# Loading the values of a cross-attention kernel in runs of 80 rows per head instead of 77

## The chip, the cores and the metric

The kernel runs on one core of a Trainium2 chip. The core has a matrix engine (TensorE, "PE" in the profile; its weight loads are "PEld"), a vector engine (VectorE, "DVE"), a scalar engine (ScalarE, "ACT"), a general engine (GpSimd, "POOL"), and SyncE ("SP"), which in this kernel computes nothing and issues every DMA. Sixteen DMA engines carry the transfers. The metric is device time of one execution in microseconds (us), the median of several runs.

## The reference

Only the text part of the original block is alive: `x` is 32 batches of 512 queries with 640 channels, `ctx` is 32 batches of 77 keys with 1024 channels, and there are 20 heads of 32 channels.

```python
q = _heads(x @ to_q_w)                    # 32 x 20 x 512 x 32
k = _heads(ctx[:, :77] @ to_k_w)          # 32 x 20 x 77 x 32
v = _heads(ctx[:, :77] @ to_v_w)
p = softmax(q @ k.T / sqrt(32))           # 512 x 77 for each head
out = _merge(p @ v) @ to_out_w + to_out_b + x
```

The three other attentions of the original (object, others, image prompt) read slices of `ctx` that are empty here, so they add nothing.

## The kernel before, in words

Every matmul is made in three passes: each operand is split into a high and a low part (`split`, lines 98 to 100: ACT copies the high part, DVE subtracts it to get the low part), and high times high, high times low and low times high are added up.

**First stage, to about 289 us.** Keys and values of all 32 batches are computed (matmuls in lines 163 and 189). All 2464 rows (32 times 77) lie one behind the other. Both results go to scratch memory in DRAM: `k_dram`, and `v_dram`, which holds for each row, head and channel the high and the low part side by side. This stage's instructions, its DMAs too, are placed by the scheduler.

**Main stage.** Work is cut into 160 blocks `n = 5 b + j`: batch `b` (512 queries) and chunk `j` of four heads. `slot(n)` (line 485) writes out by hand what PE, ACT, DVE and POOL do while block `n` is the newest one in the pipeline, and the text below calls this "slot j" of a batch. In slot `n`:

- PE makes the scores of block `n` in four parts (`sc`, line 334), between them the queries of block `n+1` (`pq`, line 316), then the product of probabilities and values for block `n-3` (`pa`, line 415), then, in slots 2, 3, 4 and 0 of a batch but not in slot 1, the output projection of a quarter of an earlier batch (`po`, line 442).
- ACT makes the 16 exponentials of block `n` (`pn`, line 352), the high parts of queries and results (`qt`, `at`, line 99), the high part of the probabilities of block `n-2` (`pp`, lines 395 and 399), and in slots 3 and 0 of a batch the high parts of `x` (`xt`, line 267).
- DVE takes maxima (`nm`, line 342), low parts (`pp`, line 396; line 100), and transposes blocks of 32 by 32 (`z`, line 371). POOL normalizes (`pn`, line 364), makes further low parts (`pp`, line 400; `xt`, line 268) and adds the bias to the residual (`xr`, line 437).

The probabilities have queries on partitions and must have keys there. The transposed blocks `z` go to a DRAM buffer `pd` in four DMAs (line 378), and come back as `raw` in two (lines 387 and 388). There is **one** `raw` buffer: the load for a block can only be issued when POOL and DVE have finished with the block before it, and when that block's four `pd` stores have landed. `split_p` then makes `pp` from `raw`: ACT line 395, DVE line 396, ACT line 399, POOL line 400. `pa` consumes `pp`.

**The values.** A head's 77 keys are padded to 80 in `pn` (the three columns stay zero), so four heads fill 320 rows: two tiles of 128 and one of 64. `vb` holds the values in the same layout, as a block diagonal in three tiles; it is cleared once. `SEGMENTS` (lines 35 to 43) lists for each tile which rows of which head go there: runs of 77, 48, 29, 77, 16 and twice 61 rows (the last run is stored twice, for the high and for the low part of the probabilities). `load_values(b, g)` (line 298) issues one DMA for each run, for two chunks (`g = 0`) or three (`g = 1`); a row and chunk is 256 bytes. It is called from `refill`, behind the `pa` of slots 2 and 4. `load_keys` fetches `kb` likewise, in four DMAs.

**Order of the DMAs.** All DMAs go through one queue, SP's, which takes them one after the other and waits in front of each for what it needs. A DMA also waits until the one eight places ahead of it has landed, because completion semaphores are used in turn. Up to slot 7, SP's order is the program's; from slot 8 on the scheduler places SP's instructions by its own estimate of times, while the other engines keep the order written in `slot`. In steady state the order of one batch is, from slot 0: `kb` x4, `vb` x7 of `g = 0`, `xr`, `raw` x2, `out`, `pd` x4, `xr`, `raw` x2, `out`, `pd` x4, `xr`, `kb` x4, `vb` x2 of `g = 1`, `raw` x2, `pd` x4, `vb` x5, `out`, and on to slots 3 and 4.

Of the kernel before, what the change touches and what calls it, by code (L numbers as in the profile page):

```python
# [8 lines left out]
F32 = mybir.dt.float32  # L9
FPR = mybir.dt.float32r  # L10
# [12 lines left out]
P = 128  # L23
Q = 32
HEADS = 20
HD = 32
NKEY = 77
HPC = 4
KCOLS = HPC * NKEY
KPAD = 80  # L30
# [5 lines left out]
for _t in range(3):  # L36
    for _i in range(HPC):
        _lo = max(_t * P, _i * KPAD)
        _hi = min((_t + 1) * P, _i * KPAD + NKEY)
        if _lo < _hi:  # L40
            SEGMENTS.append((_t, _lo - _t * P, _i, _lo - _i * KPAD, _hi - _lo))
            if _t == 2:
                SEGMENTS.append((_t, _lo - _t * P + 64, _i, _lo - _i * KPAD, _hi - _lo))
# [6 lines left out]
def kernel(  # L50
# [24 lines left out]
    nc = tc.nc  # L75
    B, S, C = x.shape
    CA = ehs.shape[2]
    NT = B * NKEY
# [11 lines left out]
    dram = ctx.enter_context(tc.tile_pool(name="scratch", bufs=1, space=DRAM))  # L90

    k_dram = dram.tile([P, NC_, 2, NT], FPR, name="k_dram")
    v_dram = dram.tile([NT, HEADS, HD, 2], FPR, name="v_dram")
    wo_dram = dram.tile([P, NC_, 2, C], FPR, name="wo_dram")

    bias = const.tile([P, C], F32, name="bias")
# [111 lines left out]

    zero = kvt.tile([P, G], FPR, name="zero", tag="craw")
    nc.vector.memset(zero.bitcast(F32), 0.0)  # L210
    warm = psk.tile([P, G], F32, tag="ps", name="warm")
    for _ in range(12):
        nc.tensor.matmul(warm, zero[:, :P], zero, start=True, stop=True)
# [473 lines left out]
```

## Time and profile before

The median is 2141.44 us over three runs (2139.94 to 2143.78). The profiled execution took 2144.53 us by itself; its span, from the first to the last instruction, is 2142.8 us, at a mean granted TensorE clock of 0.985.

| what | us | share of the span |
| --- | --- | --- |
| PE busy | 2020.4 | 94% |
| PE weight loads busy | 1793.9 | 84% |
| ACT busy | 1359.8 | 63% |
| DVE busy | 1337.6 | 62% |
| POOL busy | 1094.8 | 51% |
| DMA queue of SP, share of 16 engines | | 71.5% |

Matmuls overlap in the pipeline, so a busy PE is not yet a PE at its peak. A row of waits reads: engine, tile and line that waited, what ended the wait, then us in total, number of waits and the longest. A row of the timeline reads: start and duration in us, engine, line, operation, tile written and tile read, how many instructions are merged, and in brackets the engine's idle time in front of it with what ended it. "SPq" is SyncE's queue issuing a DMA; its duration is the time to issue, waiting included, not the transfer.

### The profile page before, as it was taken

The page shows a single profiled execution, that of the slowest core. Times are in us where ns is not written, and L with a number is a line of the kernel's source. Part 1 is how long each engine was busy: PE and PEld are TensorE (multiplying, and loading weights), DVE is VectorE, ACT ScalarE, POOL GpSimd, SP SyncE. Part 2 cuts the span into 40 slices and gives each one's busy share as a digit, 9 for nine tenths or more (in the row PEclk, how much of TensorE's full clock was granted, in tenths as well). Part 3 has the DMA queues.
Part 4 walks back from the last instruction along what each step waited for, and adds up shares of the span by engine and source line. Part 5 has one row for each costly group of instructions (what it writes and reads, how often), then busy time and mean ns, then how long its engine had stood idle before and what let it go on. Part 6 is the DMA issues. An engine that isn't in the chain of part 4 may idle for free.

```text
span 2142.8 us, 36233 instructions
## 1 busy us (share of the span) xinstructions
PE 2020.4 (94%) x11012; PEld 1793.9 (84%) x11012; DVE 1337.6 (62%) x1872; ACT 1359.8 (63%) x6057; POOL 1094.8 (51%) x618
## 2 busy tenths in 40 slices
PE   8899995899999999999999999999999999999997
PEld 7799974788888888888888888888888888888886
DVE  5433244467677677666667666767767767666663
ACT  3321145577677777677767777767777677777662
POOL 0000043456656566665666665656656656666653
PEclk9999998899999999999999999999999999999998
DMA  7953265677777777777777777777777777777664
GB/s 190 266 181 115 92 138 148 192 200 205 205 206 206 209 202 204 199 213 213 211 201 202 211 211 198 204 200 207 206 197 206 206 212 206 208 202 201 189 186 129
DMA packets 524241, 416.43 MB, mean 194 GB/s; under 512 B 138480, under 2 KB 427760, under 8 KB 524048
## 3 DMA queue, kind: packets, MB, share of 16 engines
q1 hardware_dynamic: 524048, 414.13, 71.5%
q8 instruction: 88, 1.44, 0.3%
q14 instruction: 105, 0.86, 0.1%
HBM read 238.69 MB, written 175.31 MB: 193 GB/s over the span
## 4 chain that ended last, share of the span: by engine, by line
DMA 30%; ACT 23%; PE 19%; SPq 10%; issue 8%; DVE 7%; POOL 3%; DVEq 0%; POOLq 0%; ACTq 0%
ACT pn L352 14%; DMA pd<-z 12%; DMA raw<-pd 8%; DMA xs<-in_x_dram 6%; PE pk L163 5%; PE pv L189 5%; ACT pp L395 3%; PE po L442 3%; SPq L378 3%; SPq L303 3%; DVE nm L342 2%; PE pq L316 2%; PE pa L415 2%; SPq L433 2%; DVE z L371 2%
## 5 line engine op out<-in xcount | busy, mean ns | idle before, releaser
L352 ACT ACTIVATE pn<-sc,nm 128x77 f32<-128x77 f32 x2560 | 814.2, 363 | 295.9 <-DVE nm L342 295.8
L316 PE MATMUL pq<-xt,wq_s 128*128 128x512 f32 x2400 | 639.1, 396 | 10.0 <-POOL xt L268 8.9
L364 POOL TENSOR_TENSOR pn<-pn,rs 128x1232 f32<-128x1232 f32 x160 | 387.0, 2419 | 471.2 <-DVE rs L363 424.9
L352 ACT ACTIVATION_READ_ACCUMULATOR pn<-sc,nm 128x1 f32 x2560 | 620.5, 243 | 0.0
L442 PE MATMUL po<-wo_s,at 128*128 128x320 f32 x3840 | 587.8, 310 | 3.5 <-DVE xr L458 2.1
L442 PEld LDWEIGHTS po<-wo_s,at 128*128 128x128 f32 x3840 | 569.3, 188 | 7.3 <-DVE xr L458 2.9
L316 PEld LDWEIGHTS pq<-xt,wq_s 128*128 128x128 f32 x2400 | 429.9, 189 | 76.4 <-POOL xt L268 11.6
L396 DVE TENSOR_TENSOR pp<-raw,pp 128x1024 fp32r<-128x1024 f32 x160 | 307.0, 1919 | 228.2 <-ACT pp L395 228.1
L334 PE MATMUL sc<-kb,qt 128*128 128x308 f32 x1920 | 389.5, 309 | 27.3 <-ACT qt L99 20.7
L415 PE MATMUL pa<-pp,vb 128*128 128x512 f32 x1280 | 343.4, 405 | 59.4 <-DVE pp L396 33.8
L334 PEld LDWEIGHTS sc<-kb,qt 128*128 128x128 f32 x1920 | 327.0, 189 | 85.6 <-ACT qt L99 28.4
L400 POOL TENSOR_TENSOR pp<-raw,pp 64x512 fp32r<-64x512 f32 x160 | 295.6, 1848 | 156.3 <-ACT pp L399 137.1
L415 PEld LDWEIGHTS pa<-pp,vb 128*128 128x128 f32 x1280 | 244.7, 198 | 132.8 <-DVE pp L396 53.2
L395 ACT CAST pp<-raw 128x1024 fp32r<-128x1024 f32 x160 | 174.9, 1093 | 214.1 <-DMA raw<-pd 211.0
L342 DVE TENSOR_REDUCE nm<-sc 128x4 f32<-128x308 f32 x640 | 291.8, 460 | 7.8 <-PE sc L334 5.3
L371 DVE STREAM_TRANSPOSE z<-pn 128x1280 f32<-128x1280 f32 x160 | 240.2, 1501 | 25.5 <-POOL pn L364 23.7
L268 POOL TENSOR_TENSOR xt<-xs,xt 128x512 fp32r<-128x512 f32 x160 | 204.2, 1286 | 96.6 <-ACT xt L267 86.8
L437 POOL TENSOR_TENSOR xr<-xr,bias 128x640 f32<-128x640 f32 x128 | 201.0, 1570 | 53.1 <-DMA xr<-in_x_dram 43.5
L100 DVE TENSOR_TENSOR at<-pa,at 128x512 fp32r<-128x512 f32 x160 | 110.7, 692 | 140.8 <-ACT at L99 140.8
L100 DVE TENSOR_TENSOR qt<-pq,qt 128x512 fp32r<-128x512 f32 x160 | 110.2, 689 | 64.6 <-ACT qt L99 64.3
L163 PE MATMUL pk<-ct,wk_s 128*128 128x512 f32 (+1 forms) x600 | 137.4, 390 | 10.9 <-ACT ct L99 10.8
L189 PE MATMUL pv<-wv_s,ct 128*128 128x320 f32 (+1 forms) x960 | 142.1, 309 | 0.0
(37 smaller groups left out, 1109.9 us busy)
## 6 DMA issues: line engine op xcount, KB each, us to landing
pd<-z SPq DMA_DIRECT2D x640, 160.0 KB
raw<-pd SPq DMA_DIRECT2D x160, 512.0 KB
xs<-in_x_dram SPq DMA_DIRECT2D x128, 320.0 KB
xr<-in_x_dram SPq DMA_DIRECT2D x128, 320.0 KB
out_dram<-xr SPq DMA_DIRECT2D x128, 320.0 KB
raw<-pd SPq DMA_DIRECT2D x160, 128.0 KB
v_dram<-vs SPq DMA_DIRECT2D x19, 640.0 KB
k_dram<-ks SPq DMA_DIRECT2D x20, 512.0 KB
```

Source lines behind the costliest of these rows:

```text
L163: nc.tensor.matmul(pks[j][:, :gn], wk_s[:, k, a, j * P : (j + 1) * P], cts[k][:, c, :gn], start=(k == 0 and n == 0), stop=(k == NK - 1 and ...
L189: nc.tensor.matmul(pv[:tn, :HALF], cts[k][:, a, t0 : t0 + tn], wv_s[:, k, c, h * HALF : (h + 1) * HALF], start=(k == 0 and n == 0), stop=( ...
L316: nc.tensor.matmul(pqs[n], wq_s[:, k, a, j * P : (j + 1) * P], xts[b, k][:, c, :], start=(k == 0 and m == 0), stop=(k == NC_ - 1 and m == 2),)
L334: nc.tensor.matmul(sc[:, :KCOLS], qt[:, a, t * P : (t + 1) * P], kb[:, c, :], start=(m == 0), stop=(m == 2),)
L342: nc.vector.tensor_reduce(nm, sc[:, :KCOLS].rearrange("p (h k) -> p h k", k=NKEY), AX.X, ALU.max, negate=True)
L352: nc.scalar.activation(pnb[n % 2][:, at, :NKEY], sc[:, i * NKEY : (i + 1) * NKEY], AF.Exp, bias=nm[:, i : i + 1], accum_out=sms[n][:, at : ...
L364: nc.gpsimd.tensor_tensor(pf, pf, rs.unsqueeze(2).to_broadcast([P, NQ * HPC, NKEY]), ALU.mult)
L371: nc.vector.transpose(z.rearrange("p b t j -> p t b j"), pn.rearrange("p (t h) k -> p t (h k)", t=NQ).rearrange("p t (b i) -> p t b i", i=Q),)
L396: nc.vector.tensor_tensor(pp[:, 2:4, :], raw[:, 0:2, :], pp[:, 0:2, :].bitcast(F32), ALU.subtract)
L400: nc.gpsimd.tensor_tensor(pp[64:, 4, :], raw[:64, 2, :], pp[:64, 4, :].bitcast(F32), ALU.subtract)
L415: nc.tensor.matmul(pas[n], vb[:, t, :, a], pp[:, c, :], start=(m == 0), stop=(m == len(PASSES) - 1),)
L442: nc.tensor.matmul(po[:, :HALF], ats[b * NC_ + j][:, a, t * P : (t + 1) * P], wos[0][:, j, c, h * HALF : (h + 1) * HALF], start=(j == 0 an ...
```

## The change

The runs of `SEGMENTS` end at the padded length, 80, in place of 77: they become 80, 48, 32, 80, 16 and twice 64 rows. The three extra rows of a run are the first three rows of the next batch, and they are multiplied by the zero columns of the probabilities. Behind the last batch there is no next one, so `v_dram` grows by three rows, and one DMA at the start writes zeros to them, from the tile `zero` that is there for warming up PE.

```diff
 for _t in range(3):
     for _i in range(HPC):
         _lo = max(_t * P, _i * KPAD)
-        _hi = min((_t + 1) * P, _i * KPAD + NKEY)
+        _hi = min((_t + 1) * P, (_i + 1) * KPAD)
         if _lo < _hi:
@@
-    v_dram = dram.tile([NT, HEADS, HD, 2], FPR, name="v_dram")
+    v_dram = dram.tile([NT + KPAD - NKEY, HEADS, HD, 2], FPR, name="v_dram")
@@
     nc.vector.memset(zero.bitcast(F32), 0.0)
+    nc.sync.dma_start(
+        v_dram[NT:].rearrange("n h d a -> (n h d a)").rearrange("(p u) -> p u", u=P).bitcast(F32),
+        zero[: (KPAD - NKEY) * HEADS * HD * 2 // P, :P].bitcast(F32),
+    )
```

The number of DMAs is the same but for the zeros. The order on ACT and POOL is the same; on DVE too; on PE six projection matmuls move ahead by a few places once, at slot 8. SP's order changes: the zeros come behind the first two DMAs of the start, and in every batch the `xr` load that stood between `vb` of `g = 0` and `raw` moves behind `raw` x2 and `out`.

## The prediction

> **What bounds the kernel now.** I read the page's busy shares first, then the waits, then the timeline of one batch.
>
> ```profile
> PE 2020.4 (94%) x11012; PEld 1793.9 (84%) x11012; DVE 1337.6 (62%) x1872; ACT 1359.8 (63%) x6057; POOL 1094.8 (51%) x618
> ...
> PEclk9999998899999999999999999999999999999998
> ```
>
> PE is the busiest by far. To see what is left above its own speed I took the distances between starts of successive matmuls in the trace: median 231 ns for `pq`, 142 for `sc`, 229.5 for `pa`, 147 for `po`. A batch has 75, 60, 40 and 120 of them: 17.3 + 8.5 + 9.2 + 17.6 = 52.7 us. It takes 55.6 us (blocks 10 to 155: 1613.5 us over 29 batches). So PE stands still for 2.97 us a batch. By slot, the excess over those medians is 0.1 in slot 0, 0.9 in slot 1 (`sc`), 1.9 in slot 2 (`pa` 1.3, `sc` 0.6), 0.0 in slot 3, 0.1 in slot 4. Only slots 1 and 2 have anything to give: 2.8 us a batch. The waits say who is behind them:
>
> ```profile
> ACT pp L395 <- DMA raw<-pd: 211.0, 77, 8.1
> ...
> PEld pa L415 <- DVE pp L396: 53.2, 44, 2.6
> ...
> PE pa L415 <- DVE pp L396: 33.8, 37, 2.3
> ...
> PE sc L334 <- ACT qt L99: 20.7, 28, 1.2
> ```
>
> PE waits for `pp` and `qt`, thus for DVE and ACT; ACT waits 211 us for `raw`. The timeline of batch 12 (slot 0 starts at 982.23, slot 1 at 993.68, slot 2 at 1001.69) shows the place:
>
> ```profile
> 985.22 1.77 POOL L400 TENSOR_TENSOR pp<-raw,pp 64x512 fp32r<-64x512 f32 x1 [2.19 <-ACT pp L399]
> 985.37 3.55 SPq L303 DMA_DIRECT2D vb<-v_dram  x7
> ...
> 988.97 2.04 SPq L433 DMA_DIRECT2D xr<-in_x_dram  x1
> ...
> 991.12 0.39 SPq L387 DMA_DIRECT2D raw<-pd  x1
> ...
> 995.81 1.05 ACT L395 CAST pp<-raw 128x1024 fp32r<-128x1024 f32 x1 [3.49 <-DMA raw<-pd]
> ...
> 1001.69 0.55 PE L334 MATMUL sc<-kb,qt 128*128 128x308 f32 x2 [0.81 <-ACT qt L99]
> ...
> 1008.37 1.90 PE L415 MATMUL pa<-pp,vb 128*128 128x512 f32 x7 [0.95 <-DVE pp L396]
> ```
>
> The `raw` buffer is free when POOL ends at 986.99, and the last of its `pd` stores landed at 986.32. Yet `raw` is issued at 991.12: SP is held up by `vb` (the last of the seven takes 1.20 us to issue) and by `xr`, which takes 2.04 us where other `xr` issues take 0.35 to 0.53 us. No landing that `xr` waits for falls there: the DMA eight places ahead, a `kb`, landed at 987.01. ACT, done with slot 0 at 992.3, stands idle 3.49 us, and is that late for slot 1 and for the `pp` of slot 2. Slot 1 has no projection, so PE needs just 7.2 us in it, and ACT cannot catch up.
>
> **Why those issues are slow.** The trace's updates of the DMA semaphores give each landing. From the end of issue, median over the batches, `vb` with `g = 1` takes: 48 rows 1.5 us, 77 rows 2.2, 16 rows 2.1, 29 rows 3.1, 61 rows **4.5**; with `g = 0`: 1.6, 1.8, 1.55, 2.1 and **3.7**. Fewer bytes take longer. The number of updates tells why: the other 1793 DMAs give 16 each, 28,688 in all. The trace holds 32,656, so 124 a batch remain for the 14 loads of `vb`. That is exactly what comes out if 48 and 16 rows use 16 DMA engines, 77 rows 11, and 29 and 61 rows one (k updates and one more where k is below 16: 4 x 12 + 4 x 16 + 6 x 2 = 124). The Trainium skill, "DMA: Bandwidth & Descriptors", section "Why a DMA increments its semaphore by 16 and not by 1", has the rule: the largest k up to 16 that divides both sides' slowest dimension. The trace agrees to the last update. A packet of 256 bytes takes 18 ns in the trace; two runs of 61 rows and three chunks are 366 packets on one engine, an estimated 6.6 us, and SP can't issue on while that engine's queue is full.
>
> **The change part by part.**
>
> *Runs of 80, 48, 32, 80, 16, 64, 64 rows*: all divide by 16, so all use 16 engines. The seven of `g = 0` are 768 packets, 48 an engine, 48 x 18 ns = 0.9 us. Issue: seven at 0.3 to 0.42 us (the rows of 48, 77 and 16), 2.7 us in place of 3.55 in the printed row, and `xr` without its 2.04. The padding adds 75 packets a batch, 75 x 18 ns / 16 = 0.08 us of DMA, hidden: DMA engines are busy 71.5%.
>
> *`raw` ahead of `xr` and `out`*: in batch 12 it goes out at 985.37 + 2.7 = 988.1 in place of 991.12, 3.0 us earlier; in batch 9 (7.91 after slot 0's start, `vb` from 2.23) 2.9 earlier, in batch 18 (8.58, `vb` from 2.60) 3.2. It waits for its eighth predecessor, the last `kb`, landed at 987.01, and for POOL at 986.99; both are over. `xr` goes to 989.5 and lands before 993; it is wanted by POOL two slots later (26 us after slot 0's start): hidden.
>
> *Walk from there*: landing takes 3.5 (the low quarter) to 4.2 us; I take 4.0 from the end of issue: 992.4. ACT is free at 992.3, so its wait goes and all that follows on ACT is 3.3 us earlier. In batch 9's terms (slot 1 at 11.45, slot 2 then at 18.65): ACT `pp` at 10.4 and not 12.59; `pp` 1.66 and `xt` 1.24, exponentials from 13.3, `qt` at 16.6, complete at 17.9, before 18.65: the `sc` stall goes. The next `raw` waits for POOL (13.9, was 16.05) and for `pd` (its four go out from 6.8, were 9.54; landed about 12, were 15.69), lands about 18; ACT ends slot 1 at 18.96, DVE's `pp` (2.75 us) ends at 22.8, and `pa`, which needs it from its second matmul at 23.6, doesn't wait. So 2.8 us go; margins are 0.7 to 0.8 us, so I leave 0.3 us a batch as residue: 2.5 us. Batches 2 to 31 have the pattern: 30 x 2.5 = **75 us**.
>
> *Once, in slot 9*: there `vb` (398.41 on) is followed by a `raw` issue of 2.92 us at 403.36, landing at 409.84; with 2.7 us for `vb` it goes out at 401.1 and lands at about 405.2. PE's wait of 7.31 us for `xt` at 415.44 hangs on it: **4.6 us**. Slots 5 and 6 (32 us of stalls) keep theirs: SP waits there for POOL, not for `vb`.
>
> *Zeros*: third on SP at the start. They wait for the memset (0.91 to 1.39), when SP is busy with the first two anyway, and cost one issue, 0.45 us, and a place among eight: up to 2 us if the fourth `cs` must wait for the first landing (4.49). I take **1 us** lost, as the first keys hang on `cs`. PE's six moved matmuls: their inputs are ready (`at` complete at 391.4), nothing.
>
> Two rules for the whole. "DMA: Bandwidth & Descriptors", "Rules for kernel authors", says that transfers under 64 KB pay mostly overhead; all of `vb` is under 58 KB. By that rule the runs would land as before, and the change be worth 0. The row is against it: 45.8 KB in runs of 61 land in 4.5 us, 57.8 KB in runs of 77 in 2.2. I go by the row.
>
> Sum: 75 + 4.6 - 1 = 79 us. The profiled execution itself was 2144.5, so it would be 2065.5; from the median of the runs, 2141.4, **2062 us**.
>
> **The rivals.**
> *Half the gain (17 in 100)*: ACT or DVE becomes the bound in slot 1. ACT needs 8.56 us from one `pp` to the next there, PE 7.2. For it: margins of 0.8 us, and `raw` landing times reach 5.3 us at the upper quarter over all slots. If `raw` lands 1.5 us later than I say, half of the 2.8 us stays: 30 x 1.4 + 2.3 - 1 = 43 us, 2098 us. Against: nothing slow lies ahead of it any more.
> *No change (5 in 100)*: `raw` isn't held by `vb` at all, or the new runs don't spread; then 2141 us. Against: two conditions are over 4 us before the issue.
> *Slower (7 in 100)*: PE, now without pauses, is granted less clock. Half clock for 3.4 us (the unit in which the trace grants it) costs 1.7 us; more than 1.6 such a batch outweigh 2.65 us gained. Three a batch give 5.1, and 30 x 2.45 = 74 us slower: 2215 us. For it: nothing in a row. The trace has clock 0.5 in 342 to 421 and at 2097, next to stalls, and 1.0 from 80 to 342 where PE is full. The skill's "TensorE: Matmul & The Clock Gate", Part 1, says the same way round that idleness throttles; only a power limit would do it.
>
> **How the numbers follow.** The full gain has 71 in 100. Its own range: all stalls of slots 1 and 2 gone (84) and slot 9's 9.9 gone gives 2047; twice my residue and nothing in slot 9 gives 2076. The range runs down to 2044 and up to 2108, past the half-gain case. Faster by over 0.2% (about what a measurement can tell): 71 + 17 = 88; same 5; slower 7.
>
> **What would show it.** Landing of the 64-row runs falls from 4.5 and 3.7 us to about 2; updates per DMA become 16 throughout, 3,520 more packets of 4 bytes and 2,400 more of 256, so the queue's 524,048 packets become about 530,000. The `xr` issue of 2 us vanishes, `raw` follows `vb` at once, ACT's wait for `raw` falls from 211 us to under 110, PE's waits for `pp` from 87 us to under 20, a batch takes 53 us. I am wrong if `raw` lands no earlier despite an earlier issue, if ACT's wait turns into one for `nm` or `qt`, or if the granted clock falls below 0.98.

## The result and the profile after

The changed kernel takes 2092.7 us (median of four runs, 2090.7 to 2094.4) against 2140.7 for the kernel before (four runs). The ratio is 0.9774, with a 95% interval from 0.9757 to 0.9791: 48 us, 2.3%, faster. I had forecast 2062 us and a gain of 79 us. The direction holds and the range holds the time, but only because it was drawn past the rival "half the gain"; that case came, to which I had given 17 in 100, and not the full gain with 71.

The page of the kernel after, its head and its queue:

```profile
span 2092.2 us, 36233 instructions
...
PE 2006.4 (96%) x11012; PEld 1795.0 (86%) x11012; DVE 1346.8 (64%) x1872; ACT 1363.7 (65%) x6057; POOL 1108.3 (53%) x618
...
q1 hardware_dynamic: 530013, 414.77, 73.4%
```

The span shrank by 50.6 us. By the starts of the score matmuls, 7.0 us of that lie before block 10 (4.8 of them in slot 9), 40.9 between blocks 10 and 155, and the rest behind. A batch takes 54.23 us in place of 55.64; I had forecast 53. The queue's packets are as forecast: 524,048 + 2,400 of 256 bytes + 3,520 of 4 bytes + 45 for the zeros = 530,013. So every run now uses 16 DMA engines.

The waits of the kernel after (engine, tile and line, what ended the wait, us in total, how often, the longest). The line numbers are five higher than before:

```profile
ACT pp L400 <- DMA raw<-pd: 145.6, 66, 7.8
...
PEld pa L420 <- DVE pp L401: 43.5, 35, 2.6
...
PE pa L420 <- DVE pp L401: 28.2, 32, 2.3
```

ACT waits for `raw` 145.6 us where it was 211.0; I had said under 110. PE's wait of 20.7 us for `qt` (`sc <- ACT qt`) is no longer among the larger waits. But PE still waits for `pp`: 71.7 us in the two rows, where it was 87.0. I had said under 20.

The timeline of batch 12 of the kernel after; slots 0, 1 and 2 start at 963.24, 974.69 and 981.72:

```profile
966.13 3.65 SPq L308 DMA_DIRECT2D vb<-v_dram  x7
...
969.89 0.53 SPq L392 DMA_DIRECT2D raw<-pd  x1
...
975.09 1.05 ACT L400 CAST pp<-raw 128x1024 fp32r<-128x1024 f32 x1 [1.66 <-DMA raw<-pd]
...
983.66 1.16 ACT L400 CAST pp<-raw 128x1024 fp32r<-128x1024 f32 x1
...
984.85 2.76 DVE L401 TENSOR_TENSOR pp<-raw,pp 128x1024 fp32r<-128x1024 f32 x1 [0.68 <-ACT pp L400]
...
986.51 0.40 PE L420 MATMUL pa<-pp,vb 128*128 128x512 f32 x1
```

ACT's idle time before the first `pp` is 1.66 us (3.49 before), and slot 1 takes 7.03 us, which is all PE's own. But the second `pp`, for the `pa` of slot 2, starts at 983.66 and DVE ends it at 987.61, while PE has come to `pa` at 986.51 and can do only the one matmul that needs no low part.

This table is worked out from the traces: medians over batches 2 to 30, in us. "Time" is the median of the kernel's own runs; the kernel before, run beside each of them, had medians from 2139.7 to 2147.3, so small differences are to be read from the ratios below. "`raw` landed" is the landing of the first of the two loads. "PE's stalls" are the excess over the matmul distances of the prediction, a mean for a batch. "Issue behind vb" is how long SP took to issue the DMA next behind the seven `vb` of `g = 0`.

| kernel | time | `raw` issued, from slot 1's start | `raw` landed | ACT `pp`, from slot 1 | ACT `pp`, from slot 2 | stalls slot 1 | stalls slot 2 | issue behind `vb` |
|---|---|---|---|---|---|---|---|---|
| before | 2140.7 | -3.15 | 1.80 | 1.88 | 2.67 | 0.90 | 1.92 | 2.00 |
| after | 2092.7 | -4.99 | -0.55 | -0.48 | 2.16 | 0.04 | 1.38 | 0.53 |
| only 61 to 64 | 2092.5 | -5.29 | -0.83 | -0.67 | 2.00 | 0.05 | 1.35 | 0.53 |
| 61 kept, others 80 and 32 | 2155.7 | -2.78 | 2.43 | 2.50 | 2.68 | 1.39 | 1.91 | 2.11 |
| 78 | 2096.6 | -5.30 | 0.39 | 0.47 | 2.14 | 0.05 | 1.43 | 0.44 |
| 79 | 2228.8 | -1.58 | 3.36 | 3.44 | 2.68 | 2.28 | 1.95 | 0.36 |
| no `vb` loads | 2090.5 | -6.57 | -2.31 | -1.47 | 1.93 | 0.04 | 1.27 | |

### The profile page after: what moved, and what is told of

It is laid out like the page before. It is cut to its first block, busy times and chain, and to the rows that moved or that the text cites. A ratio compares the mean times of both kernels' runs of the same rounds, so it can differ in the third digit from the quotient of the medians.

```text
span 2092.2 us, 36233 instructions
## 1 busy us (share of the span) xinstructions
PE 2006.4 (96%) x11012; PEld 1795.0 (86%) x11012; DVE 1346.8 (64%) x1872; ACT 1363.7 (65%) x6057; POOL 1108.3 (53%) x618
## 4 chain that ended last, share of the span: by engine, by line
PE 34%; ACT 23%; DMA 19%; DVE 8%; issue 6%; SPq 5%; POOL 3%; DVEq 0%; POOLq 0%; ACTq 0%
ACT pn L357 16%; DMA pd<-z 10%; PE po L447 9%; PE pq L321 6%; PE pk L164 6%; PE pv L190 5%; PE pa L420 5%; DMA xs<-in_x_dram 4%; DMA raw<-pd 4%; PE sc L339 3%; ACT pp L400 3%; SPq L383 3%; DVE pp L401 3%; DVE nm L347 3%; DVE z L376 2%
## 5 line engine op out<-in xcount | busy, mean ns | idle before, releaser
L369 POOL TENSOR_TENSOR pn<-pn,rs 128x1232 f32<-128x1232 f32 x160 | 393.9, 2462 | 464.5 <-DVE rs L368 392.6
L357 ACT ACTIVATION_READ_ACCUMULATOR pn<-sc,nm 128x1 f32 x2560 | 610.5, 239 | 0.0
L401 DVE TENSOR_TENSOR pp<-raw,pp 128x1024 fp32r<-128x1024 f32 x160 | 314.6, 1966 | 170.2 <-ACT pp L400 169.8
L339 PE MATMUL sc<-kb,qt 128*128 128x308 f32 x1920 | 376.6, 306 | 2.7 <-DVE qt L101 1.5
L405 POOL TENSOR_TENSOR pp<-raw,pp 64x512 fp32r<-64x512 f32 x160 | 300.7, 1879 | 106.4 <-ACT pp L404 94.1
L400 ACT CAST pp<-raw 128x1024 fp32r<-128x1024 f32 x160 | 175.4, 1096 | 145.6 <-DMA raw<-pd 145.6
```

The source lines that it names most:

```text
L339: nc.tensor.matmul(sc[:, :KCOLS], qt[:, a, t * P : (t + 1) * P], kb[:, c, :], start=(m == 0), stop=(m == 2),)
L357: nc.scalar.activation(pnb[n % 2][:, at, :NKEY], sc[:, i * NKEY : (i + 1) * NKEY], AF.Exp, bias=nm[:, i : i + 1], accum_out=sms[n][:, at : ...
L369: nc.gpsimd.tensor_tensor(pf, pf, rs.unsqueeze(2).to_broadcast([P, NQ * HPC, NKEY]), ALU.mult)
L400: nc.scalar.copy(pp[:, 0:2, :], raw[:, 0:2, :])
L401: nc.vector.tensor_tensor(pp[:, 2:4, :], raw[:, 0:2, :], pp[:, 0:2, :].bitcast(F32), ALU.subtract)
L405: nc.gpsimd.tensor_tensor(pp[64:, 4, :], raw[:64, 2, :], pp[:64, 4, :].bitcast(F32), ALU.subtract)
```

## The experiments

**Which of the runs matters?** Two kernels pad one half of the runs each.

```diff
-        _hi = min((_t + 1) * P, (_i + 1) * KPAD)
+        _hi = min((_t + 1) * P, _i * KPAD + (KPAD if _i == 3 else NKEY))
```

> Only the two runs of 61 rows become 64; 77 and 29 stay, the zeros stay. Theory (runs on one DMA engine hold SP and raw): the two runs of 61 are 244 of 302 one-engine packets of g = 0, so most of the gain comes, 2095 to 2110 us. Rival (every run counts alike, 3 rows each): two of seven runs, 2125 us or more. The scheduler gives this kernel the changed order (raw ahead of xr).

Measured: 2092.5 us, ratio 0.9747 (0.9721 to 0.9772). All of the gain comes from the two runs of 61, and more than I expected: the loads of 77 and 29 rows, on 11 engines and one, cost nothing that can be measured beside them.

```diff
+        _hi = min((_t + 1) * P, _i * KPAD + (NKEY if _i == 3 else KPAD))   # all but the last runs
```

> The other half: 77 and 29 rows become 80 and 32, the two last runs stay 61. The scheduler gives it the old order. Theory: at most 10 us faster than before, as 244 packets on one engine stay: 2130 to 2142 us. Rival (every run counts alike): 2105 to 2115 us.

Measured: ratio 1.0032 (1.0009 to 1.0055); the kernel before, run beside it, ranged from 2140.5 to 2157 us, so the ratio is to be read and not the medians. No gain, and a loss of 0.3% that I hadn't expected. The table shows it: the DMA behind `vb` still takes 2.11 us to issue, and `raw` goes out 0.37 us later than before. The timeline has the two rows of the hold:

```profile
988.09 3.99 SPq L308 DMA_DIRECT2D vb<-v_dram  x7
992.12 1.76 SPq L438 DMA_DIRECT2D xr<-in_x_dram  x1
```

The rival "every run counts alike" falls in both experiments.

**Is it the divisor or the length?** Here the runs end at 79 rows, one short of the change.

```diff
-        _hi = min((_t + 1) * P, (_i + 1) * KPAD)
+        _hi = min((_t + 1) * P, _i * KPAD + 79)
```

> Runs end at 79 rows: 79, 48, 31, 79, 16, 63, 63. Theory (number of engines is the largest divisor up to 16): 79 and 31 take one engine, 63 takes 9; 378 packets of g = 0 on one engine in place of 302, about 1.4 us more, so no gain or slower than before, 2140 to 2190 us. Rival (longer runs or reads over the batch's end help by themselves): near the 80-row kernel, 2093 to 2105 us.

Measured: 2228.8 us, ratio 1.0385 (1.0354 to 1.0416). Two rows more for a head than before and one fewer than in the change, and 136 us slower than the change. The updates of the semaphores fit one engine for 79 and 31 rows and nine for 63; a load of 79 rows and three chunks lands 5.2 us after its issue, one of 63 rows in 1.8. I had expected at most 2190: I counted the packets but not that the one-engine runs now stand first, and fill the queue while SP still has other runs to issue. SP's rows of one batch:

```profile
1019.21 5.99 SPq L308 DMA_DIRECT2D vb<-v_dram  x7
1025.24 0.40 SPq L438 DMA_DIRECT2D xr<-in_x_dram  x1
1025.75 0.39 SPq L392 DMA_DIRECT2D raw<-pd  x1
...
1030.52 1.05 ACT L400 CAST pp<-raw 128x1024 fp32r<-128x1024 f32 x1 [3.28 <-DMA raw<-pd]
```

Seven issues take 5.99 us, because the 48-row and the 16-row load (median 1.65 and 2.15 us to issue) stand behind runs of 79; `xr`, now behind runs of 63, goes out in 0.40. So a hold falls on whatever is issued next behind the one-engine runs, `vb` itself included.

**The spread or the order?** The change also moved `raw` ahead of `xr` in the scheduler's order. So did the kernel with only 61 turned to 64; the other two kept the old order. Runs of 78 rows (13, 16, 15, 13, 16, 2 and 2 engines) keep it too.

```diff
-        _hi = min((_t + 1) * P, (_i + 1) * KPAD)
+        _hi = min((_t + 1) * P, _i * KPAD + 78)
```

> Runs end at 78 rows: 78, 48, 30, 78, 16, 62, 62, so by the divisor rule 13, 16, 15, 13, 16, 2 and 2 engines. The scheduler gives it the old order (xr ahead of raw), so this is a spread by itself. Theory (spread): the two last runs put 124 packets of g = 0 on each of two engines in place of 302 on one, so SP is held less: 2100 to 2125 us. Rival (the changed order does it): 2138 to 2145 us.

Measured: 2096.6 us, ratio 0.9797 (0.9773 to 0.9821), more than I expected. With `xr` still ahead of `raw`, two engines in place of one for the last runs give nearly all of the gain. The order rival falls: its part, with what 16 engines add to two, is at most the few us between 2096.6 and 2092.7, and the intervals overlap. The same rows of SP as in the timeline of the prediction, now with runs of 78:

```profile
967.00 3.94 SPq L308 DMA_DIRECT2D vb<-v_dram  x7
970.98 0.59 SPq L438 DMA_DIRECT2D xr<-in_x_dram  x1
971.68 0.39 SPq L392 DMA_DIRECT2D raw<-pd  x1
```

The issue of `xr` behind `vb` has gone from 2.00 to 0.44 us (medians).

A second try at equal order wrote SP's order by hand to the end, with runs of 77 and of 80:

```diff
-    with tc.manual_schedule(engines=ENGINES):
+    with tc.manual_schedule(engines=ENGINES | {mybir.EngineType.SP}):
         for n in range(LATE + 4, N):
             slot(n)
```

> The kernel before with SP's order written by hand from slot 8 on as well (the program's order: kb, vb, raw, xr, out, pd in slot 0), so that it can be compared at equal order with the next. Theory (spread frees SP and raw): 2120 to 2150 us, since raw already follows vb directly but stands behind one-engine runs. Rival (the gain is the order, raw ahead of xr): as fast as the changed kernel, 2090 to 2100 us.

> The same order, written by hand, with the change. Theory: faster than the same order with runs of 77 by 30 us or more. Rival (order): within 8 us of it.

Measured: 2539.4 and 2460.6 us. My figure for the first was far off: in program order SP stands longer in front of `raw`, waiting for POOL (316.5 us in all, 55.0 in the kernel before) and for the landing of the `pd` stores (240.6 us, 58.7 before), and PE stalls over 13 us a batch, 7.6 of them in slot 0 and 4 to 7 in slot 4. At equal order the runs of 80 are 79 us faster, as the theory has it and the order rival does not. But most of that lies in other stalls than those of slots 1 and 2, and the granted clock differs too (0.927 and 0.940), so this is weaker evidence than the runs of 78. A third kernel with the hand order put the `vb` loads behind `raw` and `xr`:

```diff
-        for m in taken:
-            refill(m)
@@ at the end of slot
+        for m in taken:
+            refill(m)
         if j == 3 and b + 2 < B:
             load_x(b + 2)
```

> As the hand order with runs of 80, but each vb load stands behind raw and xr, not in front. If what is left in slot 2 comes from the 3.6 us that seven issues take ahead of raw: 20 to 35 us faster than the hand order before it, and slot 2's stall of about 1.4 us goes below 0.6. Rival (ACT's own work in slot 1 and DVE's slow pp bound slot 2): the same within 8 us.

Measured: 2449.5 us, 11 us less than the hand order before it, and slot 2's stall falls only from 1.32 to 1.18 us a batch. That is between the two expectations, and not decisive in a kernel held up elsewhere.

**What did the zeros cost?**

```diff
-        _hi = min((_t + 1) * P, (_i + 1) * KPAD)
+        _hi = min((_t + 1) * P, _i * KPAD + NKEY)
```

> The change without its longer runs: three more rows in the DRAM tensor and the DMA of zeros at the start, runs of 77. The scheduler gives it the old order. Both theories: 2140 to 2143 us, the zeros cost 0 to 2 us.

Measured: 2141.6 us, ratio 0.998 (0.9962 to 0.9997). The DMA of zeros costs nothing that can be measured.

**Where did the other half go?** The theory of my prediction says that `raw` is held by `vb`'s issues. Then without any `vb` load the stall of slot 2 must go. This kernel leaves out the value loads of all batches but the first.

```diff
-        if bv + 1 < B and jv in (1, 4):
+        if bv + 1 < 1 and jv in (1, 4):
```

> The changed kernel with the value loads of all batches but the first left out (its output uses the first batch's values throughout). SP's scheduled order otherwise like it. If vb's issues ahead of raw are what is left: slot 2's stall goes below 0.5 us, 2055 to 2070 us. Rival (ACT and DVE bound slot 2, stall not under 1.06 us): 2080 to 2090 us.

Measured: 2090.5 us, ratio 0.9764 (0.9748 to 0.978). That is the changed kernel's time. `raw` now goes out 6.57 us before slot 1 (after: 4.99), and the `pp` that ACT makes from it, for slot 1's `pa`, waits for it in none of the 29 batches. The next `raw` lands 0.77 us into slot 2 (median); still ACT's `pp` starts 1.93 us into slot 2, and the stall is 1.27 us. So the changed kernel has taken all that the `vb` loads could give, and what is left has another cause. Its timeline, with slot 1 from 973.51 and slot 2 from 980.55:

```profile
973.54 2.09 DVE L401 TENSOR_TENSOR pp<-raw,pp 128x1024 fp32r<-128x1024 f32 x1
...
975.55 0.47 DVE L347 TENSOR_REDUCE nm<-sc 128x4 f32<-128x308 f32 x1
...
976.11 0.33 ACT L357 ACTIVATE pn<-sc,nm 128x77 f32<-128x77 f32 x1 [1.32 <-DVE nm L347]
...
980.13 1.02 PE L339 MATMUL sc<-kb,qt 128*128 128x308 f32 x6
...
980.75 0.48 DVE L347 TENSOR_REDUCE nm<-sc 128x4 f32<-128x308 f32 x1 [0.87 <-PE sc L339]
...
981.26 0.33 ACT L357 ACTIVATE pn<-sc,nm 128x77 f32<-128x77 f32 x1 [0.35 <-DVE nm L347]
...
982.49 1.05 ACT L400 CAST pp<-raw 128x1024 fp32r<-128x1024 f32 x1
...
983.57 2.75 DVE L401 TENSOR_TENSOR pp<-raw,pp 128x1024 fp32r<-128x1024 f32 x1 [0.68 <-ACT pp L400]
...
985.34 0.40 PE L420 MATMUL pa<-pp,vb 128*128 128x512 f32 x1
...
986.38 0.98 PE L420 MATMUL pa<-pp,vb 128*128 128x512 f32 x3 [0.64 <-DVE pp L401]
```

The first three of the six `sc` matmuls at 980.13 are slot 1's last. Only then can DVE take the maximum, and ACT make four exponentials; `pp` stands behind them in ACT's order. From the last scores to the end of DVE's `pp` is a chain of 0.48, 1.23 (982.49 less 981.26), 1.05 and 2.75 us with small gaps; PE gets from slot 2's start to `pa` in 4.79 us. In other slots a projection of 4.4 us (30 matmuls of 147 ns) lies between last scores and next slot; slot 1 has none. With this order of work it is a floor of 1.06 us a batch: 12 of 29 batches of the changed kernel show 1.06 to 1.09, no batch less.

The rest of slot 2's stall comes from the start of slot 1. There ACT's first exponentials wait for `nm`, and DVE takes that `nm` only behind its own `pp` (the first three rows). In 14 of the 29 batches of the changed kernel ACT still reaches slot 1's last exponentials as early as PE's scores allow. In the other 15 it comes to them up to 0.9 us later, without a pause; in 14 of these the first exponentials had begun later than in any of the 14 good batches. A late `raw` is only a part of that: in 5 of the 15 the `pp` for slot 1's `pa` did not wait for it on ACT, and without `vb` loads 11 batches are still above the floor. That is read from the traces; no run here put `nm` ahead of `pp` on DVE, or `pp` ahead of the last exponentials on ACT.

**Can `pa` be put later?** If `pp` is that late, `pa` put further back in slot 2 must find it ready.

```diff
+        defer = j == 2 and n >= 10 and live and bool(out_of)
-        if taken:
+        if taken and not defer:
             values(taken[0])
@@ the same for split_a and refill; in the projection
                     project(po[:, h], bb, t, h, j0, j1)
+                    if defer and (h, j0) == (0, 0):
+                        take(taken[0])
+                        refill(taken[0])
```

> The changed kernel with slot 2's pa (from block 10 on) moved on PE behind the last scores and the first 12 projection matmuls, 2.2 us later. If what is left (1.4 us a batch in slot 2) is that pp stands on ACT behind the last exponentials of slot 1, which wait for PE's scores, then pa finds pp ready: 2050 to 2062 us. Rival (the stall moves on to the projections that need this pa's result, or to slot 3): 2085 to 2095 us.

Measured: 2129.7 us, ratio 0.9955 (0.9936 to 0.9973). The `pa` stall of slot 2 is gone (0.00 us). That agrees with the cause but does not prove it, as a move of 2.2 us would hide any delay of this size. And 2.27 us of stall stand at the projection now, which needs this `pa`'s `at`. The rival's account came true, and at a higher price than it named. The waits of this kernel:

```profile
PEld po L447 <- ACT at L100: 55.1, 30, 2.1
PE po L447 <- ACT at L100: 47.2, 30, 1.9
```

The same move without the longer runs:

> The same move of pa in the kernel before, runs of 77. Slot 2's pa stall of 1.3 us goes here too, but the late raw still keeps ACT back in slot 1: its sc stalls (0.75 and 0.56 us) stay. Theory: 2100 to 2125 us, slower than the changed kernel with the same move by 45 us or more. Rival (the move alone makes late raw harmless): within 15 us of it.

Measured: 2168.2 us, ratio 1.0125 (1.0096 to 1.0155), 38 us slower than with them. I had expected 2100 to 2125 for lack of the projection's stall, and 45 us or more between the two. The late `raw` keeps a price under another order of PE: `sc` stalls of 0.36 and 0.32 us stay in slots 1 and 2, about half of what they were. Not all of the 38 us is `raw`: the kernel with runs of 77 also had 34 us more at half clock (last section), which is an estimated 17 us of time lost if PE was busy throughout.

A smaller move puts `pa` behind the slot's last scores only, three matmuls later.

```diff
-        if taken:
+        if taken and j != 2:
             values(taken[0])
         if live:
             s = scores(n, 3)
+        if taken and j == 2:
+            values(taken[0])
```

> The changed kernel with slot 2's pa moved on PE by three matmuls only, behind the last scores of the slot (0.43 us later); at keeps its place on ACT. If slot 2's stall is the distance from slot 1's last scores to pp on DVE, it shrinks by just that shift, from 1.38 to about 0.95 us a batch: 30 x 0.43 = 13 us, 2080 us. Rival (at, 0.43 us later on ACT, delays what follows as in the larger move): 2093 us or more.

Measured: 2088.6 us, ratio 0.9763 (0.9749 to 0.9776); the changed kernel has 0.9774 (0.9757 to 0.9791), so the two can't be told apart. It is also between my expectation (2080) and the rival (2093 or more). The `pa` stall fell from 1.15 to 0.61 us, by the shift of 0.43 and a little more; 0.49 us stand at `po`, which had 0.08. None of the runs is clearly better than the changed kernel.

## Why the prediction was right and wrong

*What holds SP.* Right. The divisor rule gives the number of engines, the packet count fits to the last packet, and the runs of 61 rows hold what is issued behind them: 2.00 us before, 0.44 with two engines at the same order. Runs of 64 land 1.5 and 1.6 us after issue (3.7 and 4.5 before). That SP is held because the one engine's queue is full is inferred; the runs show the hold, and that it goes when a run lies on two engines or more.

*`raw` goes out 3.0 us earlier.* Mis-sized: 1.8 us (from -3.15 to -4.99), and it lands 2.4 us earlier where I had 3.3. The hold of 2.0 us went, but the seven issues take 3.66 us from first to last (3.36 before), where I had reckoned 2.7: runs of 64 rows take 0.61 us to issue, runs of 80 0.43, and the 48-row load, the same in both kernels, 0.44 in place of 0.35. I had taken durations of loads of 77 and 48 rows for all of them.

*Slot 1's stall goes.* Right: from 0.90 to 0.04 us a batch.

*"ACT ends slot 1 at 18.96", so `pa` of slot 2 doesn't wait.* This is the step that failed. I let ACT run its 8.56 us of slot 1 from an earlier start, as if its work were there. But the exponentials need `nm`, which DVE takes from PE's scores, and this sets a limit at both ends of the slot.

At the end, the last quarter of the scores comes when slot 1 ends on PE. With no `vb` load at all ACT's `pp` begins 1.93 us after that, at 20.58 in the prediction's count (18.65 + 1.93). DVE starts 1.08 us later and takes 2.75, so it ends at 24.4 and not at 22.8, too late for `pa` at 23.6; slot 2 keeps at least 1.06 us.

At the start, I had the exponentials at 13.3, right behind ACT's own `pp` and `xt`. In the changed kernel ACT waits there for `nm`, 0.98 us on average (0.17 before). The rows of the two profiles, before and after:

```profile
ACT pn L352 <- DVE nm L342: 295.8, 188, 3.9
```

```profile
ACT pn L357 <- DVE nm L347: 311.5, 204, 2.8
```

They add up all slots. In slot 1 alone the wait for `nm` rose from 0.18 to 1.09 us a batch. This is one of the signs that the prediction named for being wrong: ACT's wait for `raw` turned in part into one for `nm`.

The half-gain rival named ACT as the bound of slot 1, and its result (2098 us) came close. That was luck in part: its reason was a `raw` that lands later than I had reckoned. It did land about 1 us later, but without `vb` loads it lands another 1.8 us earlier (-2.31 in the table), and the time stays the same.

*The sum.* 30 batches at 2.5 us, 75 us, was too much: 1.41 us a batch, 30 x 1.41 = 42. Slot 9: 4.6 forecast, 4.8 measured. Zeros: 1 us forecast, none measured. Moved PE matmuls: no stall.

*The rivals.* No loss of clock: 0.985 before and after, and no half clock between 430 and 2040 us in either. By the rule of the Trainium skill ("DMA: Bandwidth & Descriptors", "Rules for kernel authors") that transfers under 64 KB pay mostly overhead, the change would have been worth nothing; 48 us came, and the measurement decides.

## What to carry to other kernels

Look at the row count of every DMA, not at its bytes: a run of 61 or 79 rows ran on one DMA engine here, and it cost not itself but the next DMA in the same queue, and then whoever waits for that one; 62 rows were nearly as good as 64. When a late input is taken away, don't shift the whole of an engine's work forward: go through it and ask for each piece when its own input is made, as it is often made by the engine that one wants to speed up. The experiment that leaves the suspected work out altogether says at once how much there is to win.

## What was not expected of the hardware

- How long SP takes to issue a DMA depended on the runs around it: the same load of 48 rows and two chunks took 0.35 us behind a run of 77 rows, 0.37 behind 78 and 0.44 behind 80. Why is not settled.
- When `pa` was moved, single gaps of 1.6 to 2.1 us on PE came with stretches of half clock in the middle of the run (430 to 2040 us): seven of 3.4 us (23.8 us in all) with runs of 80, and 17 (57.8 us in all) with runs of 77. Each stretch came a few us behind such a gap, but only 7 of 29 gaps over 1.5 us were followed by one with runs of 80. In the kernel before, with no gap over 1.22 us there, none came. That part of the slowdown comes from the clock is likely, but was not tested by itself.
- DVE's `pp` takes from 1.23 to 2.75 us. The long ones, that of slot 2 among them, overlap POOL's normalizing by 1.67 us; but one in each batch overlaps it by 1.12 us and takes only 1.47, so why they are long is not settled. The one of slot 2 is in the chain that sets the floor; moving POOL's work away from it was not tried.
